# Another order of the rows of x across the partitions, and another order of the work before the first gather, in a graph layer's kernel

## The chip, the cores and the metric

The kernel runs on one core of one Trainium2 chip. The metric is the device time of one execution in microseconds (us), taken as the median of several runs. Lower is better.

## The reference

12,500 nodes have rows of 128 numbers, and 400,000 edges, sorted by `dst`, have one of two types. For each edge the source row is multiplied by the matrix of the edge's type; the results are summed by destination; a third matrix is applied to the node's own row; then come relu, a residual and a layer norm.

```python
msg = where(etype == 0, x[src] @ W_data.T + b_data, x[src] @ W_ctrl.T + b_ctrl)
agg = segment_sum(msg, dst, 12500)
out = layernorm(x + relu(agg + x @ W_self.T + b_self))     # eps 1e-5, no scale or shift
```

## The kernel before

The edges are cut into 3,125 chunks of 128, and 125 chunks make a group (25 groups). In a group, windows of 20 chunks ("e") alternate with windows of 5 or 25 ("p"). There are 107 e-windows. This text calls an e-window with its work a *set*, numbered from 0. Source rows are fetched in two ways at once:

- **p-windows by gathers.** GpSimd issues one indirect DMA for each chunk (`msg<-rows`, line L828), which fetches 128 rows from a table in DRAM, `rows3`. A row of the table is a row of x as three bf16 parts (768 bytes). A left-over gather for each pair of sets (`both<-rows`, L905) fetches what a set could not hold.
- **e-windows by TensorE.** The same three parts lie in SBUF as `x3` (128 partitions x 98 columns x 3 x 128). A set sorts its 2,560 edges into 100 cells of 32 places, a cell for each column of x3: VectorE makes a 0/1 matrix of the columns (`O`, L533), TensorE counts along it (`side`, L622), VectorE makes ranks of the counts (`ahead`, `prod`, `found`, `rank`, `rm`, `rv`: L630 to L674), and TensorE puts lanes and codes in their cells (L686). ScalarE copies the result (`cell`, L694), which goes to DRAM and comes back broadcast to all partitions (`there`, `pick`: L697, L699); VectorE turns it into 0/1 (`pick`, L741). Then TensorE picks rows: `got<-x,pick` (L930), 98 matmuls for a set, whose moving side is a column of x3. ScalarE copies them to bf16 (`emsg`, L944).

Either way TensorE adds the rows to the destinations by a 0/1 matrix (`esel`, `psel`: L533; `sums`: L755), VectorE adds the sums to an accumulator (`acc`, `cnt`: L817), and finished nodes go through the weights, the norm and out.

**Which node lies where.** In the kernel before, node n lies in partition n mod 128 and column n div 128 of x3. So a set takes an index apart by a shift and a mask (`then`, once for each of 25 groups):

```python
nc.vector.tensor_single_scalar(parts[:, 0, :], idx, 7, op=OP.logical_shift_right)    # L511, column
nc.vector.tensor_single_scalar(parts[:, 1, :], idx, 127, op=OP.bitwise_and)          # L512, lane
```

**The work ahead of the first gather.** x is loaded in 8 pieces (`xt`, L281, 14 columns each but the last two), on ScalarE's DMA queue. A piece is split in three by ScalarE (a copy, L287, and two activations, L289) and scaled by VectorE (`power`, L291, and a multiply, L294). It is then stored to the table by SyncE's queue (`rows<-x`, L301). No gather can start before the whole table is stored. Meanwhile VectorE makes constant tables and the ranks of sets 0, 1 and 2, and TensorE picks the rows of set 0, which needs only x3. SyncE's queue also carries the indices of the groups (L246), the first destinations of the windows (`first_e`, `first_p`, L255, ten small transfers), weights and biases (L324 to L328), `first_all` (L456) and every set's `there` and `pick`, but those of set 0, which GpSimd issues.

**What sets the order.** The code emits pieces of work at positions between 0 and 1 of a set, merged by position (`merged`, `evenly`), and a scheduler orders each engine's instructions from that. Each engine and each DMA queue runs its instructions in that order, and one that waits holds up those behind it. `tc.issue_after(i)` puts the instructions of a block behind `i` in the order of `i`'s engine; it is no wait by itself. The code ahead of the loop is:

```python
    ready = [u() for u in prep(0)][-1]                                               # L1137
split_units.pop(0)()
merged([(1.5, lambda: places_after(parted[2]))],
       evenly(all_slots(0) + all_slots(1)), evenly(split_units))                     # L1139
merged(pick_matrix(0))
for u in begin_slots(2): u()
store_rows()                                                                         # L1148
spare_rows(0)                                                                        # the first gather
with tc.issue_after(placed[0].ins):
    load(1)
    load_near()                                                                      # first_all
```

Of the kernel before, what the change touches and what calls it, by code (L numbers as in the profile page):

```python
# [19 lines left out]
P = 128  # L20
# [24 lines left out]
NBLK = -(-N // P)  # L45
NQ = 25
# [5 lines left out]
AHEAD = 14  # L52
FAR = -(-PW // DPC)
# [102 lines left out]
def row_tables(nc, keep, tmp):  # L156
# [21 lines left out]
    nc.vector.tensor_single_scalar(pick_first, pick_first_cols(nc, tmp, col), 0.0, op=OP.is_equal)  # L178
# [16 lines left out]
def pick_first_cols(nc, tmp, col):  # L195

    cols = tmp.tile([P, 3, GC], FP, name="cols")
# [6 lines left out]
    return cols  # L204


def short_path(ctx, tc, const, ident, eps, wT, brow, bad, x, src, dst, etype, ws, bs, out):
# [52 lines left out]
    load_first("e")  # L260
    load_first("p")

    early, pro = ExitStack(), ExitStack()
    parted = []
# [4 lines left out]
    def split_x(pool):  # L269

        tiles, units = {}, []
        pieces = [(b, min(step, NBLK - b), P) for b in range(0, NBLK, step)]
        b, m, _ = pieces.pop()
        pieces += [(b, m - 1, P), (b + m - 1, 1, N - (NBLK - 1) * P)]

        def at(t, b, m, rows):
            return t[b * P:b * P + (m - 1) * P + rows, :].rearrange("(k p) d -> p k d", p=rows)

        def fetch(b, m, rows):
            t = tiles[b] = pool.tile([P, step, D], FP, name="xt")[:rows, :m, :]  # L280
            nc.scalar.dma_start(out=t, in_=at(x, b, m, rows))  # L281

        def split(b, m, rows):
# [3 lines left out]
            nc.scalar.copy(part[:, :, 0, :], t.bitcast(BF).rearrange("p k (d b) -> p k d b", b=2)[:, :, :, 1])  # L287
            for j in range(2):
                nc.scalar.activation(part[:, :, 2 - j, :], byte[:, :, :, j], AF.Copy, scale=2.0 ** (8 * j - 23))  # L289
            power = pool.tile([P, step, D], BF, name="power", bufs=2)[:rows, :m, :]  # L290
            nc.vector.tensor_single_scalar(  # L291
                power.bitcast(I16), part[:, :, 0, :].bitcast(I16), -128, op=OP.bitwise_and
            )
            parted.append(nc.vector.tensor_tensor(  # L294
                part[:, :, 1:, :], part[:, :, 1:, :],
                power.rearrange("p k (j d) -> p k j d", j=1).to_broadcast([rows, m, 2, D]), op=OP.mult,
            ))

        def store():
            for b, m, rows in pieces:  # L300
                nc.sync.dma_start(  # L301
                    out=at(rows3, b, m, rows), in_=x3[:rows, b:b + m].rearrange("p k j d -> p k (j d)")
                )

        ahead = 4
        for p in pieces[:ahead]:
            fetch(*p)
        for k, p in enumerate(pieces):
            def unit(k=k, p=p):
                with tc.issue_after(ready.ins):  # L310
                    split(*p)
                if k + ahead < len(pieces):
                    fetch(*pieces[k + ahead])
            units.append(unit)
        return units, store

    split_units, store_rows = split_x(pro.enter_context(tc.tile_pool(name="pro", bufs=4)))
# [5 lines left out]
    for i, (w, b) in enumerate(zip(ws, bs)):  # L323
        nc.sync.dma_start(out=wn[:, i, :], in_=w)  # L324
        row = b.rearrange("(o d) -> o d", o=1)
        nc.sync.dma_start(out=brow[:, i, :], in_=row)
        at = (0, CAP, PARTS)[i]
        nc.sync.dma_start(out=bias[at:at + PARTS, :], in_=row.to_broadcast([PARTS, D]))  # L328
# [36 lines left out]
    for t in blks:  # L365
        nc.vector.memset(t, -1.0)
# [4 lines left out]
    for t in om_all:  # L371
        nc.vector.memset(t, 0.0)

    ltri = keep.tile([P, 4, P], BF, name="ltri")
    free, own = iota([4, P], [[P // 4, 4], [1, P]], 0, 0, "i6"), iota([4], [[P // 4, 4]], 0, 1, "i7")
# [4 lines left out]
    for a in range(4):  # L380
        tables = nc.vector.tensor_scalar(ltri[:, a, :], free[:, a, :], own_f[:, a:a + 1], None, op0=OP.is_gt)
# [5 lines left out]
    nc.vector.memset(worst, 0.0)  # L387
# [974 lines left out]
```

## Time and profile before

| | before |
|---|---|
| median of 3 runs | 1741.98 us (1740.0 to 1743.36) |
| the profiled execution's own time | 1746.84 us |
| its span | 1745.0 us |
| mean granted TensorE clock | 0.993 |
| TensorE busy | 1588.9 us, 91% |
| VectorE busy | 1555.4 us, 89% |
| ScalarE busy | 1249.5 us, 72% |
| GpSimd busy | 1266.2 us, 73% |
| first gather issued | 74.96 us after the start of the span |

In the rows that follow, PE is TensorE, PEld its weight loads, DVE VectorE, ACT ScalarE, POOL GpSimd and SP SyncE; a q behind the name is the engine's sequencer, where DMAs are issued. A row of a timeline gives start, duration, engine, line, operation, what is written and read, the shapes, and in square brackets the idle time of the engine ahead of it and what ended that. A row of the windows gives a stretch, its length, the busy time of PE, PEld, DVE, ACT and POOL, the granted clock, the DMA engines' busy share and GB/s. Line numbers are those of the kernel before.

### The profile page before, as it was taken

What the parts mean: (1) busy time and instruction counts of PE and PEld (TensorE: products, weight loads), DVE (VectorE), ACT (ScalarE), POOL (GpSimd) and SP (SyncE); (2) the same over time, 40 slices, a digit from 0 to 9 for tenths busy, and PEclk for the clock granted to TensorE, in tenths of its full rate; (3) what the DMA queues carried; (4) which work ended last, traced back from release to release, by engine and by line L of the source; (5) the groups of instructions that cost most, each with busy time, mean ns of one, the idle gap of its engine ahead of it and who ended that gap; (6) DMA issues with size and microseconds to landing.
All of it is one profiled execution on the core that took longest, in us unless ns stands there. A gap on an engine that the chain in (4) does not pass through costs nothing.

```text
span 1745.0 us, 67260 instructions
## 1 busy us (share of the span) xinstructions
PE 1588.9 (91%) x28154; PEld 1238.1 (71%) x28154; DVE 1555.4 (89%) x3677; ACT 1249.5 (72%) x2251; POOL 1266.2 (73%) x1061
## 2 busy tenths in 40 slices
PE   0599999999999999999999999999999999999997
PEld 0377777777777777777777777777777777777776
DVE  7898899999899899899998898999998898998983
ACT  5777777777777777767777777776777676777675
POOL 0277777887778777777777677787777788768772
PEclk9999999999999999999999999999999999999999
DMA  7844454544454444444545444545454545444431
GB/s 202 276 125 145 129 151 129 156 145 145 126 156 127 143 150 139 137 137 131 155 124 160 133 145 129 153 127 155 135 156 127 150 125 146 143 146 126 128 123 59
DMA packets 148966, 248.22 MB, mean 142 GB/s; under 512 B 35937, under 2 KB 115260, under 8 KB 148652
## 3 DMA queue, kind: packets, MB, share of 16 engines
q1 hardware_dynamic: 85994, 134.45, 23.4%
q0 software_dynamic: 50032, 102.98, 22.0%
q10 hardware_dynamic: 12626, 6.40, 1.4%
q8 instruction: 222, 3.64, 0.8%
q14 instruction: 92, 0.75, 0.1%
HBM read 226.24 MB, written 17.50 MB: 140 GB/s over the span
## 4 chain that ended last, share of the span: by engine, by line
PE 43%; DVE 41%; issue 8%; ACT 4%; DMA 3%; DVEq 0%; SPq 0%; POOL 0%; ACTq 0%; POOLq 0%
PE sums L755 19%; PE got L930 14%; DVE esel L533 5%; DVE prod L639 4%; PE side L1049 4%; DVE pick L741 4%; DVE rv L674 3%; DVE found L641 3%; DVE prod L634 3%; DVE prod L612 2%; DVE psel L533 2%; ACT emsg L944 2%; DVE rm L533 2%; PE side L622 2%; DVE O L533 1%
## 5 line engine op out<-in xcount | busy, mean ns | idle before, releaser
L828 POOL DMA_INDIRECT msg<-rows,idx_g x985 | 1194.3, 1213 | 349.0 <-issue 134.4
L944 ACT CAST emsg<-got 128x768 bf16<-128x768 f32 (+1 forms) x1070 | 953.4, 930 | 340.9 <-PE got L930 325.0
L755 PE MATMUL sums<-esel,emsg 128*128 128x176 bf16 x7704 | 693.6, 240 | 2.2 <-DVE acc L817 1.9
L755 PEld LDWEIGHTS <-emsg 128*128 128x128 bf16 x7704 | 566.8, 98 | 111.6 <-issue 104.2
L930 PE MATMUL got<-x,pick 128*32 128x384 bf16 x10486 | 591.9, 331 | 17.8 <-DVE pick L741 10.6
L930 PEld LDWEIGHTS <-pick 128*32 128x32 bf16 x10486 | 242.0, 96 | 139.5 <-DVE pick L741 13.8
L533 DVE TENSOR_TENSOR esel<-code_col,code 128x1760 bf16<-128x1760 bf16 x321 | 293.2, 913 | 20.4 <-PE sums L755 19.0
L755 PE MATMUL sums<-psel,msg 128*128 128x48 bf16 x2955 | 184.3, 184 | 39.8 <-DVE cnt L817 35.8
L755 PEld LDWEIGHTS <-msg 128*128 128x128 bf16 x2955 | 152.6, 97 | 72.9 <-issue 69.4
L639 DVE TENSOR_TENSOR prod<-prod 128x1200 bf16<-128x1200 bf16 x214 | 133.7, 625 | 4.7
L634 DVE TENSOR_TENSOR prod<-O,ahead 128x2000 bf16<-128x2000 bf16 x107 | 128.3, 1199 | 2.7
L533 DVE TENSOR_TENSOR O<-cell_col,blk 128x2000 bf16<-128x2000 bf16 x107 | 127.3, 1189 | 0.5 <-ACT blk L437 0.5
L817 DVE TENSOR_TENSOR acc<-acc,sums 128x176 f32 (+2 forms) x232 | 66.5, 289 | 58.2 <-PE sums L755 49.2
L741 DVE TENSOR_SCALAR pick<-pick,lane_f 128x3200 bf16<-128x3200 bf16 x107 | 112.8, 1054 | 2.8 <-DMA pick<-there 2.8
L905 POOL DMA_INDIRECT both<-rows,idx x54 | 66.5, 1231 | 61.8 <-ACT emsg L944 43.1
L686 PE MATMUL side<-rv,O 128*128 128x64 bf16 x2140 | 84.5, 195 | 21.1 <-DVE rv L674 20.0
L533 DVE TENSOR_TENSOR psel<-near_col,near 128x1200 bf16<-128x1200 bf16 x125 | 96.1, 769 | 0.0
L686 PEld LDWEIGHTS <-O 128*128 128x128 bf16 x2140 | 79.7, 100 | 23.0 <-DVE rv L674 19.8
L674 DVE TENSOR_TENSOR rv<-rm,vals 128x1280 bf16<-128x1280 bf16 x107 | 87.8, 821 | 0.0
L641 DVE TENSOR_REDUCE found<-prod 128x20 f32<-128x600 bf16 x107 | 83.0, 775 | 2.7
L612 DVE TENSOR_TENSOR prod<-O 128x1000 bf16<-128x1000 bf16 x107 | 71.9, 672 | 0.0
L630 DVE TENSOR_REDUCE ahead<-side 128x100 bf16<-128x200 f32 x107 | 38.8, 363 | 32.8 <-PE side L622 29.5
(192 smaller groups left out, 1571.8 us busy)
## 6 DMA issues: line engine op xcount, KB each, us to landing
pick<-there SPq DMA_DIRECT2D x106, 800.0 KB
msg<-rows,idx_g POOLq DMA_INDIRECT x985
acc<-acc_start SPq DMA_DIRECT2D x23, 640.0 KB
rows<-x SPq DMA_DIRECT2D x6, 1344.0 KB
xs<-in_x_dram SPq DMA_DIRECT2D x99, 62.5 KB
out_dram<-h SPq DMA_DIRECT2D x99, 62.5 KB
xt<-in_x_dram ACTq DMA_DIRECT2D x6, 896.0 KB
cnt<-cnt_start SPq DMA_DIRECT2D x22, 160.0 KB
```

The costliest lines, as they stand in the source:

```text
L533: nc.vector.tensor_tensor(sel.rearrange("p n (w t) -> p n w t", t=2), col[:rows].rearrange("p (o w t) -> p o w t", o=1, t=2).to_broadcast( ...
L612: nc.vector.tensor_add(h[:, :2 * CQ], s["O"][:, :2 * CQ], s["O"][:, 2 * CQ:])
L634: nc.vector.tensor_tensor(prod[:, :, :NCELL], s["O"], ahead.rearrange("p (o j) -> p o j", o=1).to_broadcast([P, EC, NCELL]), op=OP.mult,)
L639: nc.vector.tensor_add(prod[:, :, :h], prod[:, :, :h], prod[:, :, h:2 * h])
L641: nc.vector.tensor_reduce(found, prod[:, :, :h], AX.X, OP.add)
L674: placed[:] = [nc.vector.tensor_tensor(rv.rearrange("p c v (r t) -> p c v r t", t=2), rm.rearrange("p c (o r t) -> p c o r t", o=1, t=2).t ...
L686: nc.tensor.matmul(s["rk"][:m, :2 * CAP], s["held"][:, c * NCELL:c * NCELL + m], s["rv"][:, c].rearrange("p v r -> p (v r)"), start=(c == ...
L741: nc.vector.tensor_scalar(t, t, lane_f, None, op0=OP.is_equal)
L755: last = nc.tensor.matmul(out, msg[:, j * D:(j + 1) * D], sel, start=(start and j == 0), stop=stop, skip_group_check=True)
L828: return nc.gpsimd.indirect_dma_start(out=msg, out_offset=None, in_=rows3[:, :], in_offset=bass.IndirectOffsetOnAxis(ap=codes["p", g][0][: ...
L930: last = nc.tensor.matmul(ps[CAP * a:CAP * (a + 1), :], slots[w]["pick"][:, a * NQ + q, :], x3[:, 4 * q + a - a0].rearrange("p j d -> p (j ...
L944: s["out"] = nc.scalar.copy(msg[:, :n], ps[:, :n, :3 * D])
```

## The change

Node n now lies in partition n div 98 and column n mod 98, so that a partition holds 98 rows of x that follow each other in DRAM. Partition 127 has only 54 of them; its other 44 columns are filled with zeros by a DMA. The rest follows from that or goes with it:

- x is loaded and stored in 8 pieces of 14, 13, 14, 13 columns on 128 partitions and 14, 14, 14, 2 on 127. A transfer of 127 partitions is made as one of 112 and one of 15. What a partition moves in a transfer is one run (7,168 bytes to load 14 columns, 10,752 to store them), where it was 14 runs of 512 or 768 bytes.
- The first two pieces are loaded on ScalarE's queue, the others on SyncE's, all ahead of the small transfers; group 1's and 2's indices and `first_all` are loaded after the stores.
- Column and lane come out of a division by 98 made of three VectorE instructions in place of two.
- Set 0's ranks stand in one stretch, ahead of VectorE's part of every split. Set 0's pick matrix and its first two `esel` are made before the splits are over, and set 1's work is merged with the last part of the splits.
- Some fills move from VectorE to GpSimd, two temporary tables are smaller, and the gather of left-over rows gets a bounds check.

```diff
+FULL = N - (P - 1) * NBLK            # 54
+LATE = 68
-        pieces = [(b, min(step, NBLK - b), P) for b in range(0, NBLK, step)]
...
+        halves = [FULL // 2, FULL - FULL // 2]
+        sizes = [(n, P) for h in halves for n in (h - h // 2, h // 2)]
+        sizes += [(n, P - 1) for n in (step, step, step, rest - 3 * step)]
...
-            return t[b * P:b * P + (m - 1) * P + rows, :].rearrange("(k p) d -> p k d", p=rows)
+        def at(t, b, m, lo, n):
+            c = t.shape[-1]
+            return bass.AP(tensor=t.tensor, offset=t.offset + (lo * NBLK + b) * c, ap=[[NBLK * c, n], [c, m], [1, c]])
+        def spans(rows):
+            return [(lo, n) for lo, n in ((0, rows - rows % 16), (rows - rows % 16, rows % 16)) if n]
...
-            nc.scalar.dma_start(out=t, in_=at(x, b, m, rows))
+            for lo, n in spans(rows):
+                fetches.append(queue.dma_start(out=t[lo:lo + n], in_=at(x, b, m, lo, n)))
...
+            with tc.issue_after((first_pick if b >= LATE else first_placed).ins):
                 nc.vector.tensor_single_scalar(power..., -128, op=OP.bitwise_and)
                 parted.append(nc.vector.tensor_tensor(part[:, :, 1:, :], ..., op=OP.mult))
...
-        for p in pieces[:ahead]:
-            fetch(*p)
+        for k, p in enumerate(pieces[:ahead]):
+            fetch(*p, nc.sync if k > 1 else nc.scalar)
...
+    with tc.issue_after(fetches[-1].ins):
+        load_first("e")
+        load_first("p")
         for i, (w, b) in enumerate(zip(ws, bs)):
...
-            nc.vector.tensor_single_scalar(parts[:, 0, :], idx, 7, op=OP.logical_shift_right)
-            nc.vector.tensor_single_scalar(parts[:, 1, :], idx, 127, op=OP.bitwise_and)
+            nc.vector.tensor_scalar(place, idx, 0.5 * (1 - NBLK), 1.0 / NBLK, op0=OP.add, op1=OP.mult)
+            nc.vector.tensor_scalar(lane, place, 2.0 ** 23, -2.0 ** 23, op0=OP.add, op1=OP.add)
+            nc.vector.scalar_tensor_tensor(parts[:, 0, :], lane, float(-NBLK), idx, op0=OP.mult, op1=OP.add)
...
-            in_offset=bass.IndirectOffsetOnAxis(ap=slots[w]["idx"][:n], axis=0),
+            in_offset=bass.IndirectOffsetOnAxis(ap=slots[w]["idx"][:n], axis=0), bounds_check=N - 1, oob_is_err=False,
...
-        ready = [u() for u in prep(0)][-1]
-    split_units.pop(0)()
-    merged([(1.5, lambda: places_after(parted[2]))], evenly(all_slots(0) + all_slots(1)), evenly(split_units))
+        leading, *_, ready = [u() for u in prep(0)]
+    for u in all_slots(0):
+        u()
+    first_placed = placed[0]
+    first_pick, = [u() for _, u in pick_matrix(0)]
+    for q0, n in ((0, 10), (10, 9)):
+        made[0, q0] = node_columns(0, q0, n)
+    merged(
+        [(1.5, lambda: places_after(parted[2]))],
+        evenly(split_units, 0.0, 0.8),
+        evenly(all_slots(1), 0.45, 1.1),
+    )
...
-    merged(pick_matrix(0))
...
-    store_rows()
+    stored = store_rows()
     spare_rows(0)
-    with tc.issue_after(placed[0].ins):
+    with tc.issue_after(stored.ins):
         load(1)
         load_near()
```

More of the change, by code (lines that the diff above doesn't have):

```diff
@@ L290, in split @@
[L290 to L297, printed above, removed]
+                with tc.issue_after((ready if b or j else leading).ins):
+                    nc.scalar.activation(part[:, :, 2 - j, :], byte[:, :, :, j], AF.Copy, scale=2.0 ** (8 * j - 23))
@@ L486, in begin @@
         def begin():
-            nc.scalar.copy(sf, s)
+            return nc.scalar.copy(sf, s)
         def rows():
@@ L906, in spare_rows, with node_columns @@
             out=both[:n, :], out_offset=None, in_=rows3[:, :],
-            in_offset=bass.IndirectOffsetOnAxis(ap=slots[w]["idx"][:n], axis=0),
+            in_offset=bass.IndirectOffsetOnAxis(ap=slots[w]["idx"][:n], axis=0), bounds_check=N - 1, oob_is_err=False,
         )
+    made = {}
+    def node_columns(w, q0, n):
+        return select(sp.tile([P, 10, 2 * EW], BF, name="esel")[:, :n], code_col, slots[w]["code"][:, q0:q0 + n])
     def picked(w, tiled, ending, before):
@@ L919, in choose @@
         def choose(q0, n):
-            sel = select(sp.tile([P, 10, 2 * EW], BF, name="esel")[:, :n], code_col, slots[w]["code"][:, q0:q0 + n])
+            sel = made.pop((w, q0), None) or node_columns(w, q0, n)
             for k in range(n):
@@ L1187, in short_path @@
         if i == 3 and g + 2 < NG:
-            load(g + 2)
+            with tc.issue_after(stored.ins):
+                load(g + 2)
         tiled, begin = {}, []
```

97 lines of the change are left out of this document (59 added, 38 removed).

## The prediction

> **What bounds the kernel now.** I read the page first (shares, chain), then the windows of the stages, then the timeline from the start to set 2. From some 100 us on the kernel is in its loop:
>
> ```profile
> PE 43%; DVE 41%; issue 8%; ACT 4%; DMA 3%; DVEq 0%; SPq 0%; POOL 0%; ACTq 0%; POOLq 0%
> ...
> 30.00:40.00 10.00, 1.28 (x20) 1.15 (x20) 9.90 (x17) 10.00 (x8) 0.00 (x0) 1.00 1.06 316
> 80.00:90.00 10.00, 9.12 (x126) 5.78 (x127) 5.23 (x8) 6.36 (x10) 7.86 (x8) 0.67 0.54 167
> 400.00:800.00 400.00, 378.83 (x6757) 295.40 (x6754) 363.52 (x850) 289.33 (x533) 315.00 (x255) 1.00 0.47 141
> ```
>
> From 30 to 40 us VectorE, ScalarE and the DMA engines (share 1.06) are all full; from 80 to 90 none is, and TensorE's clock is granted at 0.67. In the loop TensorE is busy for 378.8 of 400 us and VectorE for 363.5; the chain is shared by the two. The change leaves the loop as it is but for one VectorE instruction in each group, so nearly all must come from the first 100 us. There the rows are these:
>
> ```profile
> 0.81 15.44 ACTq L281 DMA_DIRECT2D xt<-in_x_dram  x4
> 22.21 0.30 ACT L487 CAST sf<-srcs 125x128 f32<-125x128 int32 x1 [3.62 <-DMA srcs<-in_src_dram]
> 22.70 0.23 DVE L511 TENSOR_SCALAR parts<-idx_g 128x125 int32<-128x125 int32 x1 [9.97 <-ACT idx_g L505]
> 23.72 1.20 DVE L533 TENSOR_TENSOR O<-cell_col,blk 128x2000 bf16<-128x2000 bf16 x1 [0.46 <-ACT blk L437]
> ...
> 74.96 1.03 POOL L905 DMA_INDIRECT both<-rows,idx  x1 [24.93 <-ACT emsg L944]
> 80.01 0.51 ACT L992 COPY last<-both 64x384 bf16<-64x384 bf16 x1 [5.18 <-DMA both<-rows,idx]
> 81.30 0.34 DVE L817 TENSOR_TENSOR acc<-acc,sums 128x176 f32 x1 [3.43 <-PE sums L755]
> 95.79 1.04 DVE L741 TENSOR_SCALAR pick<-pick,lane_f 128x3200 bf16<-128x3200 bf16 x1
> 97.37 1.00 PE L930 MATMUL got<-x,pick 128*32 128x384 bf16 x20
> ```
>
> ScalarE issues four loads of x until 16.3, waits for group 1's indices until 22.2 (they stand ahead of set 0's in its order), and set 0's ranks begin at 23.72. The table of rows is stored by 74.96, when the first gather is issued; it is used at 80.01, and VectorE's first accumulate follows at 81.30. Set 2's pick matrix ends at 96.8 and its matmuls begin at 97.37. I compare the kernels at these last two points: what comes after is the loop in both.
>
> **Part 1: set 0 begins earlier, a gain.** The changed kernel's order on ScalarE is: two loads issued, set 0's indices, a copy and an activation of the first piece, five small copies with an activation among them, `O`. The first piece's landing and the costs:
>
> ```profile
> 0.81 7.55 DMA xt<-in_x_dram
> 28.64 1.69 ACT L287 COPY x<-xt 128x1792 bf16<-128x1792 bf16 x1
> 29.20 2.02 DVE L294 TENSOR_TENSOR x<-x,power 128x3584 bf16<-128x3584 bf16 x1
> 31.13 0.62 DVE L291 TENSOR_SCALAR power<-x 128x1792 int16<-128x1792 int16 x1
> 33.40 1.68 ACT L287 COPY x<-xt 128x1792 bf16<-128x1792 bf16 x1
> 33.90 0.67 DVE L612 TENSOR_TENSOR prod<-O 128x1000 bf16<-128x1000 bf16 x1
> 35.30 0.82 DVE L674 TENSOR_TENSOR rv<-rm,vals 128x1280 bf16<-128x1280 bf16 x1
> 53.31 1.57 ACT L287 COPY x<-xt 128x1664 bf16<-128x1664 bf16 x1
> 57.75 0.20 ACT L694 CAST cell<-side 128x64 bf16<-128x64 f32 x1
> ```
>
> A piece of 14 columns costs ScalarE 33.40 - 28.64 = 4.8 us (copy 1.6, activations 1.6 each), one of 13 columns 57.75 - 53.31 = 4.4. With the first piece in at 8.4 as before: 8.4 + 1.6 + 1.6, 1.3 for the small copies (22.7 to 23.72 and the one ahead of it), 1.6 for the second activation: `O` of set 0 starts at 14.5, 9.2 us earlier. From `O` to the end of `rv` it was 36.1 - 23.7 = 12.4 us, with other work in it; without the multiply, the `power` and the `prod` of set 1 that stand there (2.0, 0.6, 0.7) it is 9.1 undivided. `rv` ends at 23.6, TensorE's part is over by 25, and ScalarE copies `cell` behind its fourth copy, 14.5 + 4.4 + 4.8 + 1.5 = 25.2, so by 25.4.
>
> **Part 2: ScalarE then waits for set 0's pick matrix, a loss.** The built order puts the first `emsg` of set 0 ahead of the fifth piece's split:
>
> ```
> ACT: ... split of piece 4 | emsg | piece 5 | emsg | piece 6 | emsg | pieces 7, 8 | bits | cell (set 1)
> SP:  ... loads of pieces 5 to 8 | rows 1 | rows 2 | there (set 1) | rows 3 | pick | rows 4 | ... | rows 8 | group 1 | first_all
> ```
>
> Its cell goes by GpSimd's queue through DRAM. How long that takes is shown from two sides:
>
> ```profile
> 43.43 0.79 POOL L697 DMA_DIRECT2D there<-cell  x1 [38.74 <-ACT cell L694]
> 49.42 0.61 POOL L699 DMA_DIRECT2D pick<-there  x1 [5.20 <-DMA there<-cell]
> 58.22 1.05 DVE L741 TENSOR_SCALAR pick<-pick,lane_f 128x3200 bf16<-128x3200 bf16 x1
> 60.20 0.80 ACT L944 CAST emsg<-got 128x768 bf16<-128x768 f32 x1 [1.65 <-PE got L930]
> 96.81 0.28 SPq L697 DMA_DIRECT2D there<-cell  x1
> 98.83 0.35 SPq L699 DMA_DIRECT2D pick<-there  x1
> ...
> 62.00:64.00 2.00, 1.43 (x28) 0.57 (x23) 2.00 (x9) 1.97 (x7) 0.00 (x0) 1.00 1.10 375
> 66.00:68.00 2.00, 2.00 (x38) 1.48 (x38) 2.00 (x4) 2.00 (x3) 0.00 (x0) 1.00 1.07 346
> ```
>
> With full DMA engines 49.4 - 43.4 = 6.0 us passed until the second transfer was issued and 8.8 more at most until VectorE had it; with half-empty ones the first takes 2.0 us, and its 0.8 MB at 375 GB/s with 0.6 to issue at least 2.8. From 25.4 the matrix is in between 30.2 and 40.2. VectorE comes to it at about 34: three `power`, two multiplies, `O`, three smaller products and two `esel` at 0.91 (below), 10.4 us from 23.6. I take 36, the middle, as the first stores flow from 30 on. Then 1.05 us for the matrix and 0.9 until the first eight picks are done (60.20 less the end of the row at 58.22): ScalarE goes on at 38, having been free since 14.5 + 4.4 + 4.8 + 4.4 + 0.4 = 28.5. What stands before set 1's `cell` is three pieces (14.3), two columns (0.7), three `emsg` (0.8 the narrow ones, as at 60.20, and half as much again the wide one: 2.8) and 0.3: it is done at 56.1.
>
> **Part 3: the stores stand behind it.** SP's order has `there` of set 1 after the second store. SP waits there until 56.1, and six of eight stores behind it, though the third piece is ready at about 39. So 71 of 98 columns and a `pick` are left: 71 x 128 x 768 bytes and 128 x 6,400 bytes, 7.8 MB. What rate runs of 10,752 bytes reach, no row shows; the rows of the full DMA engines above have 346 to 375 GB/s, which makes 20.8 to 22.5 us, and I take 21, with 2.0 for the ends (96.81 to 98.83 is a small transfer's whole way). The first gather is issued at 56.2 + 21 + 2.0 = 79.2, against 74.96: **4.2 us later**. The earlier loads, the earlier ranks and the earlier splits are all spent by then.
>
> The Trainium skill, "DMA: Bandwidth & Descriptors", under Specifications, gives 358 GB/s as the limit of HBM for one core, by which longer runs could not help; the window at 62 us, with 375, stands above it, and by the rule the stores would take 21.7 us instead of 21. The same page's measured table has 425 GB/s for 16 MB moved into SBUF; no run here shows that, and by it they would take 18.3.
>
> **Part 4: what is done while waiting, a gain.** In the built order TensorE does 86 of set 1's 98 picks ahead of set 0's last sums, where before it did none, and VectorE has made all of set 1's `esel`. From the accumulate (81.30) to the end of set 2's pick matrix (96.83) VectorE took 15.5 us; some 3.5 of that it idled (4.8 in the window 80:90, less the 1.3 before 81.30). That wait for set 1's picks goes.
>
> ```profile
> L755 PE MATMUL sums<-esel,emsg 128*128 128x176 bf16 x7704 | 693.6, 240 | 2.2 <-DVE acc L817 1.9
> L533 DVE TENSOR_TENSOR esel<-code_col,code 128x1760 bf16<-128x1760 bf16 x321 | 293.2, 913 | 20.4 <-PE sums L755 19.0
> L817 DVE TENSOR_TENSOR acc<-acc,sums 128x176 f32 (+2 forms) x232 | 66.5, 289 | 58.2 <-PE sums L755 49.2
> L533 DVE TENSOR_TENSOR psel<-near_col,near 128x1200 bf16<-128x1200 bf16 x125 | 96.1, 769 | 0.0
> ```
>
> The changed order between the two points holds two `esel` of set 2, one `psel` and three accumulates more (1.8 + 0.8 + 0.9 = 3.5), and two `esel` of set 1 less (1.6): 12.0 + 3.5 - 1.6 = 13.9, and I give it 1 us of waits for TensorE (bounds 0 and the 3.5 of before). With the accumulate at 81.3 + 4.2 = 85.5 the matrix ends at 100.4, 3.6 late. But set 1 is over by then: some 35 short matmuls at 0.07 (693.6/7704 = 0.09 for a `sums`), 2.4 us, that came after 97.37 before, are done, and VectorE has its 3.5 us. TensorE is left 3.6 - 2.4 = **1.2 us late**, VectorE even.
>
> **Part 5: one instruction more in each group.** Column and lane took two, and now take three, of the price of these:
>
> ```profile
> L512 DVE TENSOR_SCALAR parts<-idx_g 128x125 int32<-128x125 int32 x21 | 5.5, 263 | 0.0
> L511 DVE TENSOR_SCALAR parts<-idx_g 128x125 int32<-128x125 int32 x21 | 4.6, 217 | 0.0
> ```
>
> A middling 0.25 us for each of 24 groups makes 6 us if nothing hides it, nothing if VectorE's idle 9% does, and by VectorE's 41% of the chain **2.5 us**.
>
> **At nothing.** The fills on GpSimd (idle until 43 before), zeros for partition 127, smaller tables and the last group's count tile lie beside other work. The bounds check costs GpSimd at least nothing and at most, if it doubled the gather at 74.96 (1.03 us, 54 of them), 56 us, of an engine that idles for 85 us of each 400 in the loop; without that cover it would be 0.5 us a set. `first_all` now lands after the stores; VectorE's `first` stands in order ahead of the accumulate. It is a price that the trace doesn't show; SP may issue it while stores still flow, so I take it as covered by the gather's 5.05 us, and up to 4 us if not.
>
> **The sum** is 1.2 + 2.5 = +3.7 us. The profiled execution took 1746.84 us for a span of 1745.0; it would take 1750.5. It lies 4.9 over the median of the runs, 1741.98, so the median becomes **1746 us**. A difference of under 0.2% (3.5 us) can't be told from none.
>
> **The rivals.** *Faster: TensorE alone binds.* It enters the loop with nearly all of set 1 done, 13 of the 15 us that a set takes (1,645 us after the first 100 for 105 sets). If VectorE clears its 13.9 us while TensorE would be waiting anyway, the gain is 13 less the 4.2 and the 2.5: -6, or 1736. For it: VectorE's idle 3.5 us after 81.3. Against: both engines run in a fixed order, and set 2's picks need that pick matrix. It decides if the matrix is done before 94. Also here falls a pick matrix that lands by 33, with stores at more than 400 GB/s: -3 and -2, 1741 with the rest. Chance 0.25.
>
> *Slower by more.* Set 0's matrix lands at 40 (all later by 4), or `first_all` comes 4 us after the gather: 1750; with the full 6 of part 5, 1754. For it: the first stores and the last load flow at just that time, and `first_all` stood ahead of the stores before and stands behind them now. Chance 0.20.
>
> *No difference.* The third instruction falls in idle time, and part 4 is even: 1742. Chance 0.15.
>
> *The layout does nothing for the transfers.* Then the first piece still lands at 8.4, which is my sum, 1746. Were it in three us sooner, parts 1 to 3 would come at most as much sooner, 1743. Both are in my own case.
>
> My own case has 0.40; of it 0.27 lies over 0.2% and 0.13 within. So faster 0.25, same 0.28, slower 0.47. The range reaches from the faster rival to the slower one: 1736 to 1754.
>
> **What would show it.** Right: `O` of set 0 near 14.5; an idle ScalarE of 8 to 10 us ahead of the first `emsg`; no `rows<-x` issued between 33 and 55; the first gather near 79; set 2's picks near 100; afterwards a loop of the same pace. Wrong: the third store issued before 50, or the first gather before 74, would break part 3; set 2's picks before 96 would break part 4; a loop whose 400 us hold other counts of work would break part 5.

## The result and the profile after

The changed kernel took 1767.93 us (median of 4 runs, 1765.28 to 1769.3) where the kernel before took 1742.67 beside it (1740.0 to 1745.67): the ratio is 1.0151, with a 95% interval of 1.0137 to 1.0165. The forecast was slower, 1746, with a range from 1736 to 1754; the loss is 25 us instead of 4. The profiled execution took 1767.29 us for a span of 1765.5, so 20.5 us over the span before.

Line numbers are from here on those of the kernel that a row comes from. The windows of the changed kernel (busy us of TensorE, its weight loads, VectorE, ScalarE and GpSimd with the instructions in brackets, granted TensorE clock, DMA share, GB/s):

```profile
0.00:120.00 120.00, 51.47 (x598) 32.33 (x598) 85.86 (x233) 68.35 (x94) 28.19 (x46) 0.88 0.61 195
30.00:40.00 10.00, 0.63 (x12) 0.52 (x12) 5.76 (x8) 0.91 (x1) 0.95 (x1) 1.00 1.02 356
70.00:80.00 10.00, 5.68 (x83) 3.82 (x80) 8.89 (x19) 6.30 (x10) 0.00 (x0) 1.00 1.02 401
80.00:90.00 10.00, 9.56 (x131) 5.58 (x120) 0.98 (x1) 7.12 (x9) 0.00 (x0) 0.83 0.73 210
110.00:120.00 10.00, 7.13 (x80) 3.98 (x80) 7.24 (x28) 5.47 (x17) 5.10 (x5) 0.50 0.50 158
400.00:800.00 400.00, 377.45 (x6701) 293.94 (x6701) 362.87 (x850) 286.76 (x524) 312.17 (x252) 1.00 0.47 141
```

From 400 us on the loop carries 6701 matmuls in 400 us, 6757 before: nearly the same pace (Part 5 below comes back to the 56). In the first 120 us it is another kernel. ScalarE and VectorE, full from 30 to 40 us before, are now idle for 9 and 4 of these 10 us, and from 80 to 90 VectorE does one instruction. The same first window of the kernel before:

```profile
0.00:120.00 120.00, 58.38 (x917) 41.98 (x917) 99.28 (x267) 80.84 (x111) 40.55 (x51) 0.97 0.72 212
```

By 120 us TensorE has done 598 matmuls instead of 917. The loop does 16.9 in a microsecond (6757 / 400), so the 319 that are missing are 18.9 us of it: nearly the whole 20.5. Rows picked from the engines' timelines show where they went (start, duration, engine, line; in brackets the idle time ahead and what ended it):

```profile
17.08 1.20 DVE L561 TENSOR_TENSOR O<-cell_col,blk 128x2000 bf16<-128x2000 bf16 x1 [0.75 <-ACT blk L461]
27.64 0.20 ACT L723 CAST cell<-side 128x64 bf16<-128x64 f32 x1
...
42.95 1.05 DVE L770 TENSOR_SCALAR pick<-pick,lane_f 128x3200 bf16<-128x3200 bf16 x1 [7.18 <-DMA pick<-there]
44.94 0.80 ACT L979 CAST emsg<-got 128x768 bf16<-128x768 f32 x1 [14.03 <-PE got L965]
62.67 0.21 ACT L723 CAST cell<-side 128x64 bf16<-128x64 f32 x1
63.30 0.32 SPq L315 DMA_DIRECT2D rows<-x  x1
78.44 1.05 DVE L770 TENSOR_SCALAR pick<-pick,lane_f 128x3200 bf16<-128x3200 bf16 x1
87.04 0.98 DVE L561 TENSOR_TENSOR esel<-code_col,code 128x1584 bf16<-128x1584 bf16 x1 [7.47 <-PE sums L784]
90.92 0.71 DVE L561 TENSOR_TENSOR esel<-code_col,code 128x1056 bf16<-128x1056 bf16 x1 [2.90 <-PE sums L784]
91.31 1.29 POOL L934 DMA_INDIRECT both<-rows,idx  x1 [55.43 <-ACT sf L511]
95.09 0.51 ACT L1027 COPY last<-both 64x384 bf16<-64x384 bf16 x1 [3.78 <-DMA both<-rows,idx]
96.11 0.29 DVE L485 CAST first<-first_all 125x25 f32<-125x25 int32 x1 [4.48 <-DMA first_all<-in_dst_dram]
97.95 0.66 DVE L493 TENSOR_SCALAR near_all<-side,from_of 125x25 f32<-125x25 f32 x3 [1.55 <-PE side L488]
101.12 0.34 DVE L846 TENSOR_TENSOR acc<-acc,sums 128x176 f32 x1 [2.51 <-ACT code L745]
111.39 0.68 PE L528 MATMUL side<-ident,code_r 125*128 125x125 f32 x2 [6.64 <-DVE code_r L518]
113.39 1.05 DVE L770 TENSOR_SCALAR pick<-pick,lane_f 128x3200 bf16<-128x3200 bf16 x1
114.49 1.79 PE L965 MATMUL got<-x,pick 128*32 128x384 bf16 x20 [0.27 <-DVE pick L770]
```

Two stretches of waiting are to be seen. For set 0's pick matrix VectorE waits 7.2 us and ScalarE 14.0, with x's pieces behind them. And from set 1's pick matrix (78.44) to the first accumulate (101.12) VectorE waits five times, 7.47 + 2.90 + 4.48 + 1.55 + 2.51 = 18.9 us. TensorE pays for it behind the accumulate: at 111.39 it has waited 6.64 us for `code_r`, VectorE's preparation of group 1, which stands there. Set 2's pick matrix ends at 114.4, where it ended at 96.8 before: 17.6 us of the 20.5 are lost by then. (The gather's wait is put down to `sf`; in the program it is for the stores, whose data flow until just ahead of it.)

### The profile page after: what moved, and what is told of

The parts are those of the page before. It is cut to its first block, busy times and chain, and to the rows that moved or that the text cites. A ratio compares the mean times of both kernels' runs of the same rounds, so it can differ in the third digit from the quotient of the medians.

```text
span 1765.5 us, 67352 instructions
## 1 busy us (share of the span) xinstructions
PE 1601.1 (91%) x28154; PEld 1241.8 (70%) x28154; DVE 1563.2 (89%) x3695; ACT 1250.4 (71%) x2251; POOL 1277.1 (72%) x1067
## 3 DMA queue, kind: packets, MB, share of 16 engines
q0 software_dynamic: 50032, 102.98, 21.7%
## 4 chain that ended last, share of the span: by engine, by line
DVE 43%; PE 39%; issue 9%; ACT 6%; DMA 2%; DVEq 1%; POOL 0%; SPq 0%; ACTq 0%; POOLq 0%
PE sums L784 17%; PE got L965 13%; DVE esel L561 5%; DVE pick L770 4%; DVE prod L668 4%; PE side L1084 3%; DVE rv L703 3%; DVE found L670 3%; DVE prod L663 3%; DVE prod L641 2%; ACT emsg L979 2%; DVE psel L561 2%; DVE rm L561 2%; PE side L651 1%; DVE O L561 1%
## 5 line engine op out<-in xcount | busy, mean ns | idle before, releaser
L934 POOL DMA_INDIRECT both<-rows,idx x54 | 70.5, 1306 | 94.5 <-ACT sf L511 56.6
L651 PEld LDWEIGHTS <-ltri 128*128 128x128 bf16 x1284 | 41.3, 97 | 38.4 <-issue 30.6
```

## The experiments

Eighteen kernels, each the changed kernel with a few lines edited unless it says otherwise; r1 is the changed kernel as it is. The table has the time, its ratio to the kernel before measured beside it, and from the profile the matmuls done by 120 us, the start of the first gather, of the first accumulate and of set 2's pick matrix. What an edit gives back is worked out from the ratios, against 1.0148, the mean of the changed kernel's two rows; 0.001 is 1.74 us.

| kernel | us | ratio, 95% interval | matmuls by 120 | gather | accumulate | set 2's matrix |
|---|---|---|---|---|---|---|
| before | 1742.67 | 1 | 917 | 74.96 | 81.30 | 95.79 |
| changed | 1767.93 | 1.0151, 1.0137-1.0165 | 598 | 91.31 | 101.12 | 113.39 |
| r1 changed, again | 1766.48 | 1.0144, 1.0119-1.0168 | 606 | 91.72 | 101.59 | 113.99 |
| r2 set 1's picks later | 1766.89 | 1.0143, 1.0117-1.0169 | 641 | 90.74 | 100.82 | 111.96 |
| s1 queue | 1760.23 | 1.0103, 1.0088-1.0117 | 696 | 76.30 | 95.01 | 107.27 |
| s2 matrix later | 1757.44 | 1.0082, 1.0066-1.0098 | 790 | 80.42 | 89.59 | 101.86 |
| t1 loads ahead | 1758.13 | 1.0102, 1.0083-1.0120 | 798 | 87.08 | 103.15 | 105.50 |
| s3 queue, matrix | 1756.97 | 1.0089, 1.0072-1.0106 | 799 | 67.95 | 88.84 | 101.11 |
| t2 matrix, loads | 1752.16 | 1.0070, 1.0051-1.0088 | 875 | 79.24 | 98.81 | 101.16 |
| t3 queue, matrix, loads | 1755.36 | 1.0078, 1.0058-1.0097 | 818 | 77.16 | 102.45 | 104.81 |
| r3 these, stores whole, fills back | 1742.85 | 1.0008, 0.9997-1.0020 | 1041 | 70.02 | 88.70 | 91.76 |
| r4 r3, set 1's picks later | 1747.86 | 1.0033, 1.0020-1.0047 | 929 | 69.97 | 88.16 | 90.41 |
| t4 r3, two multiplies on GpSimd | 1754.94 | 1.0084, 1.0066-1.0103 | 871 | 76.64 | 98.75 | 101.09 |
| s4 before, third instruction | 1743.86 | 1.0009, 0.9999-1.0018 | 992 | 72.65 | 79.39 | 91.30 |
| u1 before, the layout | 1751.35 | 1.0069, 1.0055-1.0084 | 885 | 81.58 | 96.47 | 97.95 |
| u2 u1, stores whole | 1750.60 | 1.0058, 1.0044-1.0072 | 929 | 76.86 | 84.82 | 95.26 |

### q1 to q4: four edits alone, on a chip with a slower loop

I began with the prediction's chain: set 1's cell, stores, gather, accumulate. Theory S: the loss is the stores' place behind set 1's cell on SP. Theory M: it is the wait for set 0's matrix. T: the divided stores have a tail. N: `first_all` lands late.

```
q1  queue = nc.sync if w > 1 else nc.gpsimd              # was: if w
q2  set 0's emsg: issue_after(the last split's activation)
q3  rows3: N rows -> P * NBLK rows; spans(rows) -> [(0, P)] in the stores
q4  load(1), load_near(): issue_after(fetches[-1]), ahead of store_rows()
```

> The two transfers of set 1's cells go through GpSimd's queue, so no store waits for them on SP; all else as in the changed kernel (1767.9 us). Theory S (the stores' place behind set 1's cell is the main loss): the third store is issued at about 46, when VectorE has multiplied the third piece (43.91 + 2.02 in the changed kernel), the last at 65.6 (last multiply), the first gather at 68 to 72 instead of 91.3, and 14 to 19 us of the 25 come back: 1749 to 1754. Theory M (the waits of ScalarE and VectorE for set 0's pick matrix are the main loss): they stay, so at most the 8 us by which 91.3 exceeds the byte count come back: 1760 or more. Rival: set 1's pick matrix, now under the stores, comes late and takes the gain: the gather is early, but the time falls by under 5 us.

> ScalarE does all splits of x ahead of set 0's first emsg, so it no longer waits for the pick matrix with splits behind it; SP's order is unchanged. Theory M: ScalarE goes on at 31 instead of 45, its splits are over by 48, set 1's cell follows VectorE's rv (55.71 + 0.80) and TensorE at about 58 instead of 62.7, the gather comes 4 to 5 us sooner (87) and the time falls by 4 to 5 us: 1763. If VectorE's own wait of 7.2 us for the same matrix were the whole of it, cell of set 1 stays within 1 us of 62.7 and the time too. Theory S expects no more than these 5 us from this edit alone, since six stores still stand behind the cell.

> The table of rows in DRAM has 128 x 98 rows, and the last four stores are made with 128 partitions in one transfer each instead of 112 and 15; the loads stay divided. Theory T (the transfers of 15 partitions leave some DMA engines with more than others, which is the tail in which the moved GB/s falls from 80 to 91 us): the stores end when 8 x 0.41 + 8 x 0.244 + 8 x 0.375 + 24 x 0.41 + 8 x 0.065 = 18.6 us of packets per engine are over, the gather is issued at 84 to 86 instead of 91.3, and the time falls by 5 to 6 us: 1762. Rival (the tail is contention at the memory, whatever the division): the gather stays within 2 us of 91.3 and the time within 2 us of 1768.

> Group 1's loads and first_all are issued ahead of the stores, as in the kernel before, instead of behind them. Theory N (first_all's landing, not the gather, ends the wait of VectorE at 96.1): VectorE's copy of it is done early, the accumulate follows the gather as before (74.96 to 81.30, 6.3 us) instead of after 9.8 us, so at about 97.7 instead of 101.1, and the time falls by 3 to 4 us: 1764. If group 1's other loads in the stores' tail delay the stores as well, the gather is 1 to 3 us sooner too. Rival: the accumulate waits for the gathered rows anyway, time within 1 us of 1768.

These four came to a chip on which the kernel before took 2038.79 us, and the ratios (1.0130, 1.0164, 1.0163, 1.0110, each within 0.005) settle nothing: the changed kernel was not timed there, and the loop itself ran slower. The window of q1:

```profile
400.00:800.00 400.00, 341.70 (x5663) 257.36 (x5661) 308.93 (x715) 243.73 (x443) 245.56 (x212) 0.97 0.39 118
```

5663 matmuls in 400 us, though a `sums` takes 0.24 us there as elsewhere. What held it is not shown. Of use is the time up to the gather. In q1 it is issued at 74.92, 16 us sooner, where S had 68 to 72. In q3 it comes 24.3 us after set 1's cell (62.87 to 87.14) instead of 28.6 (62.67 to 91.31), and 28.4 in q2 on the same chip (59.99 to 88.34): the divided stores have 4 of the 5 to 6 us that T gave them. In q2 ScalarE goes on without waiting, but set 1's cell comes only 2.7 us sooner, at 59.99, where M had 58: VectorE still waits for the matrix, 8.41 us. In q4 `first` runs at 73.66, and the accumulate at 105.32 is no sooner for it: against N.

### r1 to r4: the order on TensorE, and five edits together

Theory G: only the gather's time counts. Theory O: TensorE's order counts, since set 1's picks, ahead of set 0's last sums, have to wait for set 1's matrix.

```
r2  set 1's pick matmuls: issue_after(set 0's last sum)
r3  q1 + q3 + q4 + fills on nc.vector + pick_matrix(0) traced behind
    the merge of splits and set 1's ranks, pieces gated by first_placed
r4  r3 + r2
```

> The changed kernel once more, as the base line of the three runs beside it. All theories: 1.0151 times the kernel before (25 us), if the chip paces the loop as in the first runs.

> TensorE does set 1's picks, all but the first five columns, behind set 0's last sums, as in the kernel before; all else as changed. Theory O (with set 1's picks ahead of set 0's end, the accumulate has to wait for set 1's pick matrix at 78.4 and 13 us of TensorE behind it, whatever the gather does, and VectorE idles 19 us in that time): VectorE's waits at esel (7.5 and 2.9 us) go; the gather stays at 91, since the stores are unchanged, so the accumulate can come at best 6.3 us after it, at 97.6 instead of 101.1, and set 1's 13 us of TensorE come behind it: the time is within 4 us of the changed kernel's, either way. Theory G (only the gather's time counts): the accumulate 10 us behind the gather as now, set 1's work all added: 8 to 13 us slower than the changed kernel.

> Set 1's cells go by GpSimd's queue, set 0's pick matrix stands on VectorE behind set 1's ranks as in the kernel before (so neither VectorE nor ScalarE waits for it with splits behind), group 1's loads and first_all are ahead of the stores, the fills are back on VectorE, and the stores are of 128 partitions. TensorE's order is the changed kernel's. Without the 7.2 us wait VectorE is through with rv of set 2 at 70 instead of 77, set 1's pick matrix at 71 to 73, and the stores end before that. Theory G: gather at 66 to 70, accumulate 6.3 us later at 72 to 77, which is 24 to 29 us earlier than in the changed kernel, and the time is 1740 or less. Theory O: the accumulate waits for set 1's pick matrix and 13 us of TensorE: 86 to 89, and the time falls by 12 to 15 us, to 1753 to 1756, still 10 over the kernel before.

> The kernel beside it, and TensorE does set 1's picks behind set 0's last sums (all but the first five columns). Theory O: the accumulate follows the gather by 6 us, at 73 to 79, set 2's pick matrix ends at 84 to 92 where the kernel before has 96.8, and the time is 5 to 12 us under the kernel before, 1730 to 1737. Theory G: no change against the kernel beside it in the accumulate, and set 1's work comes on top: slower than it by 5 to 10 us.

r3 gives the whole 24 us back: 1742.85, no different from the kernel before. So the loss is in these five edits' reach, and the layout as such is not beyond repair. But neither theory has both: the accumulate, at 88.70, is in O's 86 to 89 and not at G's 72 to 77, while the time is not O's 1753 to 1756:

```profile
70.02 1.11 POOL L934 DMA_INDIRECT both<-rows,idx  x1 [12.22 <-DVE first L485]
...
84.11 0.33 PE L528 MATMUL side<-ident,code_r 125*128 125x125 f32 x1
86.04 0.52 ACT L1027 COPY last<-both 64x384 bf16<-64x384 bf16 x1
88.70 0.34 DVE L846 TENSOR_TENSOR acc<-acc,sums 128x176 f32 x1 [1.35 <-PE got L965]
91.76 1.04 DVE L770 TENSOR_SCALAR pick<-pick,lane_f 128x3200 bf16<-128x3200 bf16 x1
```

ScalarE's copy of the gathered rows runs 16 us after the gather without having waited for it (no bracket): it stands behind set 1's work in ScalarE's order. Set 2's matrix follows the accumulate by 3 us, 12.3 in the changed kernel, as VectorE has done set 2's and group 1's work while TensorE did set 1; TensorE doesn't wait for `code_r` (84.11, no bracket).

r2 moves nothing (1.0143 against 1.0144). O allowed that; G, by which set 1's work comes on top, had 8 to 13 us more. r4 against r3 decides against O: with set 1's picks behind, set 0's end comes no sooner (88.16), and 5.0 us are lost, which is what G gave for this run. So both theories fall, O by r4, G by r2 and r3. Having set 1's picks ahead is a credit in r3's order, as the prediction said; in the changed kernel's order, by r2, no gain shows.

### s1 to s4: the edits apart, and the third instruction

Theory V: VectorE's wait for set 0's matrix is the main loss; G and S as above.

```
s1  q1 alone
s2  pick_matrix(0) behind set 1's ranks, alone
s3  s1 + s2
s4  the kernel before, and in then():
+   nc.vector.scalar_tensor_tensor(more, idx, 256.0, idx, op0=OP.mult, op1=OP.add)
```

> Set 1's cells by GpSimd's queue, nothing else (this edit once before, where the whole loop of both kernels ran 300 us longer). The gather comes 16 us sooner, at 75, as it did there. Theory G (the gather's time is what was lost): 14 to 16 us back, 1751. Theory V (VectorE's 7.2 us wait for set 0's matrix puts set 1's pick matrix at 78, and TensorE's 13 us for set 1 stand ahead of set 0's end, so the accumulate can't be sooner than 92 or 93): 6 to 9 us back, 1758 to 1761.

> VectorE takes set 0's pick matrix behind set 1's ranks, as in the kernel before, nothing else; neither VectorE nor ScalarE then waits for it with x's pieces behind. Theory V: set 1's cell at 50 instead of 62, so the stores, which still stand behind it on SP, end 12 us sooner with their tail, gather at 78 to 80; set 1's pick matrix at 71 to 73; accumulate at 88 to 92 instead of 101; 10 to 13 us back, 1754 to 1757. Theory S (the order on SP is the main loss): at most 5 us back, 1762.

> Both edits together; first_all and group 1's loads stay behind the stores, the last four stores stay divided, the fills stay on GpSimd. Theory V: as the five edits together (1742.9) but for what first_all, the divided stores and the fills cost, which with the gather at 70 to 76 and set 1's work ending at 86 is covered: 1743 to 1747. If first_all behind the stores costs its 3.5 us here too, or the divided stores 4 us, 1747 to 1752.

> The kernel before with one more instruction of VectorE for each group (128 x 125, int32 to float, result unused), nothing else: part 5 of the prediction by itself. By the share of VectorE in the chain +2.5 us; if VectorE's idle 9% hides it, within 1 us of the kernel before; at most 24 x 0.28 = 6.7 us.

s1: the gather is 15 us sooner and only 8 us come back (0.0045), as V had it and G did not. s2: 11.5 us (0.0066), with 1757.44 at the edge of what V gave. s3 was a miss for all: the gather is 12.5 us sooner than in s2, the accumulate 0.75, the time the same. The gather's time is worth nothing there. Rows of s3, VectorE's but for one, show what is left:

```profile
71.55 1.10 DVE L770 TENSOR_SCALAR pick<-pick,lane_f 128x3200 bf16<-128x3200 bf16 x1
...
80.91 0.98 DVE L561 TENSOR_TENSOR esel<-code_col,code 128x1584 bf16<-128x1584 bf16 x1 [8.18 <-PE sums L784]
84.80 0.71 DVE L561 TENSOR_TENSOR esel<-code_col,code 128x1056 bf16<-128x1056 bf16 x1 [2.90 <-ACT sf L511]
85.42 0.17 DVE L485 CAST first<-first_all 125x25 f32<-125x25 int32 x1
86.81 0.66 DVE L493 TENSOR_SCALAR near_all<-side,from_of 125x25 f32<-125x25 f32 x3 [1.22 <-PE side L488]
88.84 0.34 DVE L846 TENSOR_TENSOR acc<-acc,sums 128x176 f32 x1 [1.36 <-PE side L736]
89.10 1.20 DVE L561 TENSOR_TENSOR O<-cell_col,blk 128x2000 bf16<-128x2000 bf16 x1
...
97.98 0.48 DVE L516 TENSOR_SCALAR rel<-dsts,near_all 125x128 f32<-125x128 int32 x2
99.11 0.68 PE L528 MATMUL side<-ident,code_r 125*128 125x125 f32 x2 [6.64 <-DVE code_r L518]
101.11 1.04 DVE L770 TENSOR_SCALAR pick<-pick,lane_f 128x3200 bf16<-128x3200 bf16 x1
```

It waits 8.18 + 2.90 + 1.22 + 1.36 us while TensorE does set 1, and only then comes to the next `O`, to group 1 (`rel`) and to set 2's matrix, while TensorE waits 6.64 us for `code_r`. No bracket of VectorE's names a transfer. What is left there lies in the order itself: `first`, and so group 1, stand behind because the planner has `first_all` behind the stores.

s4: the third instruction costs 0.0009 of the time, 1.6 us, where I had taken 2.5; the interval (-0.2 to 3.1) holds both that and nothing.

### t1 to t4: the loads' place, and an attempt to go below both

Theory Q: what counts is that VectorE gets group 1 and the next ranks in front of the first accumulate.

```
t1  q4 alone     t2  s2 + q4     t3  s3 + q4
t4  r3 + x's fifth and sixth multiply on nc.gpsimd instead of nc.vector
```

> Group 1's loads and first_all ahead of the stores in the changed kernel, nothing else (this edit once before, where the whole loop of both kernels ran 300 us longer). Theory Q (what counts is that VectorE gets group 1's preparation and set 3's ranks in front of the first accumulate, while TensorE does set 1, instead of behind it): the accumulate stays near 95 to 100, but set 2's pick matrix follows it within 5 us instead of 12, and 8 to 12 us come back: 1755 to 1759. Theory N (first_all's landing alone): 3 to 4 us back, 1763.

> VectorE takes set 0's pick matrix behind set 1's ranks, and group 1's loads are ahead of the stores; the stores still stand behind set 1's cell on SP, are divided, and the fills are on GpSimd. Theory Q: as the five edits together, within 3 us of 1743, since the gather at 78 to 80 is covered by TensorE's work on set 1 until 86. If the stores' place behind the cell matters even so: 1747 or more.

> The same with set 1's cells by GpSimd's queue, so that no store waits. Theory Q: within 2 us of 1743, so undivided stores and fills on VectorE are worth nothing there. If these two make the 14 us: 1755.

> The five edits, and the multiplies of x's fifth and sixth pieces on GpSimd, which stands idle there, instead of VectorE, which is busy from 17 to 72. VectorE loses 4 us of work: set 1's pick matrix ends at 68 to 69 instead of 73, and the time falls by 2 to 4 us under the kernel before, 1738 to 1740. If GpSimd takes over 8 us for one multiply, or VectorE runs slower beside it: no gain or up to 8 us slower, since set 1's cells stand behind them in GpSimd's queue.

t1 is as Q said: the accumulate comes even later than in the changed kernel (103.15), set 2's matrix 2.4 us after it, and 8 us come back (0.0046). VectorE's waits from set 1's matrix to the accumulate are 4.2 us instead of 18.9, and TensorE's wait for `code_r` is gone. t2 and t3 are misses for Q, 1752 and 1755 instead of 1743. They are where the other theory had them: for t2, that the stores' place matters even so (1747 or more), for t3, that undivided stores and fills make the difference (1755). Against the first speaks t3, where no store waits and which is no faster than t2. With the same loads ahead, t3 lacks only the undivided stores and VectorE's fills of r3, and is 12 us slower (0.0070). Its rows:

```profile
77.16 1.89 POOL L934 DMA_INDIRECT both<-rows,idx  x1 [17.88 <-DVE top L680]
...
99.61 1.28 PE L715 MATMUL side<-rv,O 128*128 128x64 bf16 x20 [5.44 <-DVE rv L703]
100.92 0.21 ACT L723 CAST cell<-side 128x64 bf16<-128x64 f32 x1 [6.92 <-PE side L715]
101.23 0.51 ACT L1027 COPY last<-both 64x384 bf16<-64x384 bf16 x1
```

Now the order errs to the other side: ScalarE's copy of the gathered rows, gathered at 77, stands behind the cell of a set that VectorE ranks until 99, so set 0's accumulate comes 13.8 us later than in r3, and TensorE waits 5.4 us. In the built order of r3, with four store instructions fewer, the copy stands ahead of that cell. What part of the 12 us is this, and what part the later gather (77.16 against 70.02), no run separates.

t4 is a miss: 13 us slower than r3, where 2 to 4 us were to be gained and at most 8 lost. The multiply takes 6.94 and 7.00 us on GpSimd, 2.02 on VectorE, and GpSimd's transfers for set 1 stand behind them:

```profile
42.22 6.94 POOL L307 TENSOR_TENSOR x<-x,power 127x3584 bf16<-127x3584 bf16 x1 [7.40 <-DVE power L304]
52.46 7.00 POOL L307 TENSOR_TENSOR x<-x,power 127x3584 bf16<-127x3584 bf16 x1 [3.29 <-DVE over_n L687]
59.41 0.59 POOL L726 DMA_DIRECT2D there<-cell  x1
```

No version beat the kernel before; r3 can't be told from it.

### u1 and u2: the layout in the kernel before

```
u1  the kernel before, with the changed pieces, at(), spans(), the three
    instructions and the zeros for partition 127; every load on nc.scalar
u2  u1 + q3
```

> The kernel before with the row layout only: runs of 98 rows, last four pieces in 112 and 15 partitions, three instructions for column and lane, zeros for partition 127 by a transfer; all queues, gates and merges as before. Theory W (what decides is how much TensorE has done by 120 us, 917 matmuls in the kernel before and 598 in the changed one, at 16.9 per us of the loop; the order made that, not the layout): the layout changes the planner's order little, so within 4 us of the kernel before, with 850 to 1000 matmuls by 120 us. If the layout itself lost the time: 8 us or more slower.

> The same with the last four stores undivided (128 partitions into a table of 128 x 98 rows). Seven fewer store instructions than the divided ones make the planner expect the gather sooner, and put ScalarE's copy of the gathered rows further ahead. Theory W: within 4 us of the run beside it, whichever way its matmuls by 120 us differ, 1 us for 17 of them. If divided stores cost DMA time at the gather: 3 to 5 us faster than the run beside it.

Theory W (its own count of matmuls) is wrong on the time: u1 is 11.5 us slower than the kernel before beside it (1739.81), not within 4; that is what the other theory, by which the layout itself lost the time, had (8 us or more). But it isn't only layout that it measures. ScalarE issues the loads there, and its rows show this:

```profile
29.99 5.24 ACTq L293 DMA_DIRECT2D xt<-in_x_dram  x2
35.28 3.28 ACT L301 ACTIVATE x<-xt 128x1792 bf16<-128x1792 uint8 x2 [5.12 <-DMA xt<-in_x_dram]
38.59 7.24 ACTq L293 DMA_DIRECT2D xt<-in_x_dram  x2
45.88 3.07 ACT L301 ACTIVATE x<-xt 128x1664 bf16<-128x1664 uint8 x2 [5.85 <-DMA srcs<-in_src_dram]
```

The two issues of a divided piece take 0.32 and 0.34 us each, but the second comes only 4.9 and 6.9 us after the first, and ScalarE stands idle for 5.12 + 5.85 us meanwhile, at the time when `first_all` and group 1 are issued on SP. What holds the second issue no run shows; in the kernel before these pieces had one issue each, of 0.4 to 0.6 us. The changed kernel has these loads on SP, out of ScalarE's way. So how much of the 11.5 us is the layout's stays open. u2 is within 2 us of u1, as W had it (the undivided stores are 8 instead of 12, four fewer and not seven): the division of the stores is worth at most 2 us there. Whether it is worth more between t3 and r3, where it changes the order too, or the fills are, no run shows.

## Why the prediction was wrong

**Part 1** (set 0 earlier) held in kind: `O` at 17.08 instead of 14.5, 15.5 to 15.7 in most later profiles; the cell at 27.64 instead of 25.4.

**Part 2** (ScalarE's wait) held in kind and was mis-sized. From 4.8 to 14.8 us between the cell and VectorE's having the matrix I took 10.6 (36, called the middle, which is 35.2). It was 42.95 - 27.64 = 15.3, just over the upper end, and the DMA engines were full meanwhile (share 1.02 at 356 GB/s, the window at 30 us), as in the rows that gave that end. What I left out is VectorE: I had it come to the matrix 2 us early, and it waited 7.18 with three quarters of the pieces' multiplies behind it. s2, where no piece of x stands behind that wait, gives 11.5 us back, the most of the three edits timed alone (s1, s2, t1).

**Part 3** (the stores): the order is as read, with the third store at 63.30. Set 1's cell was 62.67 instead of 56.1, and from there to the gather it took 28.6 us instead of 23.1: at 70 us the rate was better than I took (401 GB/s in that window), but the stores end in a tail, some 4 us of it by their division (q3). The Trainium skill's limit of 358 GB/s ("DMA: Bandwidth & Descriptors", Specifications) is exceeded by the trace here too, with these 401; at that limit the prediction's 7.8 MB would take 21.8 us, not 21.7. So the gather was at 91.3 instead of 79.2. Yet the gather's time is not the price: s1 takes 15 us off it for 8 us, and s3, against s2, 12.5 us for none.

**Part 4** is the step that failed: the path from the gather to set 2's matrix. I let the accumulate follow the gather by 6.3 us as before; it followed by 9.8, with `first_all` landing last, which was my "slower by more" rival. And I counted VectorE's work and waits only behind the accumulate, where they were right: 13.3 us, 13.9 + 1 forecast. I put nothing on the stretch ahead of it, called it a gain, and there VectorE waited 18.9 us. The read that was missing: in a fixed order the work that can be done while waiting must stand ahead of the wait. I credited TensorE with set 1's picks (r4: worth 5 us in r3's order) and did not ask what VectorE would do during those 13 us. It could do nothing: `esel`, `first` and the accumulate stood ahead of all its further work. t1 makes the accumulate 2 us later and the kernel 8 us faster.

Along the prediction's own chain the matrix is 14.0 us later than forecast (114.4 instead of 100.4): 6.6 by set 1's cell, 5.5 from there to the gather, 3.5 to the accumulate, less 1.6 behind it. With these sizes right the forecast would have been a loss of 18 us instead of 4, nearer the 25, but along a chain that doesn't set the time: s3 has the gather 23 us sooner than the changed kernel and gets 10 us back.

**Part 5** is not contradicted by s4: 1.6 us (-0.2 to 3.1), 2.5 forecast. The loop as a whole stays open. From 120 to 1600 us the kernel before did 25,051 matmuls and s4 25,038; the fourteen profiles with the new layout on these chips have 24,930 to 25,004, that is 3 to 7 us less work by 16.9 per us. By s4 the third instruction is at most a small part of it, and u1 and u2, without the gather's bounds check, have it too (24,991 and 24,946). What in the layout does it no run shows.

**The rivals.** Matrix at 40 and `first_all` behind the gather both came true, as "slower by more" had them, but at 1750 to 1754, each priced alone and along the same chain. "TensorE alone binds" is refuted: set 2's matrix was at 113, not before 94.

## What to carry to other kernels

Where the order of each engine is fixed, price a late input not by the step that uses it, but by all that stands behind that step on each engine, and ask of every wait what the engine has left to do ahead of it. A milestone on the old critical path (here the gather) says little when an edit changes the order: the matmuls missing by 120 us, over 16.9, with 7 us for the slower loop of Part 5, give the loss of all fourteen kernels with the new layout within 5 us. The 7 is the upper end of Part 5's 3 to 7, and it suits a profile of the kernel before that took 4.9 us over its median; counted from s4's 992, 4 us give all fourteen within 4 us. And edits of such an order don't add: 8, 11.5 and 8 us alone, 10 to 14 in twos and threes, 24 with two small ones added.

## What the hardware showed besides

Behind a transfer of 3,125 single words the next issue on its queue took long. After `first_all` it took 4.51 us in the kernel before, 7.42 in s3 and 10.29 in u1 (4.2 to 10.3 in all sixteen profiles of the table); the one behind that took 0.29, 0.34 and 3.06. In s3:

```profile
63.63 7.42 SPq L247 DMA_DIRECT2D srcs<-in_src_dram  x1
71.09 0.34 SPq L247 DMA_DIRECT2D dsts<-in_dst_dram  x1
```

A small VectorE instruction took longer beside one of GpSimd's fills. In r1, with the fills on GpSimd, the cast ends as the fill does (4.37 and 4.35); in r3, without the fills there, it takes 0.15 us:

```profile
3.60 0.75 POOL L404 MEMSET worst<- 128x640 f32 x1
3.76 0.61 DVE L167 CAST row<-row_i 128x1 f32<-128x1 int32 x1
```

```profile
5.79 0.15 DVE L167 CAST row<-row_i 128x1 f32<-128x1 int32 x1
```

The Trainium skill ("Trainium Architecture — The Big Picture", What this means for kernel authors) has the two engines share a port under an exclusive lock, and these rows fit it. It cost next to nothing in sum, as `O` of set 0 started at 15.60 and 15.51.

TensorE's clock was granted at 0.50 in the window from 110 to 120 us of the changed kernel, which begins in TensorE's wait of 6.64 us: the 20 picks at 114.49 took 1.79 us, where the same picks took 1.00 in the kernel before. How much of the loss this is no run separates.
